# Two ends of a graph-network kernel: the last pair's output by plain products, against a prologue that loads its weights early

## The chip, the cores and the metric

The kernel runs on one core of one Trainium2 chip. The core has five instruction streams that run in parallel: TensorE (PE, matrix products into the accumulator memory PSUM), VectorE (DVE), ScalarE (ACT), GpSimd (POOL) and SyncE (SP, which here only issues transfers). Each stream runs its instructions strictly in order and waits on semaphores for the others. The metric is the device time of one execution in microseconds; the figure of a kernel is the median of its runs.

## The reference

128 graphs of 128 nodes go through two layers, each with a residual and a layer norm without scale or shift. `x` is [128, 128, 512], `adj` is [128, 128, 128] with zeros and ones. Everything is float32. Cut to what matters:

```python
# layer 0: graph attention, 8 heads of 64
feats = einsum('bnf,hfu->bhnu', X, W)                       # 512 -> 8 x 64
dense = leaky_relu(e_self[..., :, None] + e_neigh[..., None, :], 0.2)
dense = dense - 1e10 * (1 - A)
out   = relu(einsum('bhij,bhju->bhiu', softmax(dense), feats) + b)
x     = layernorm(x + out)

# layer 1: hypergraph convolution twice, with a layer norm between
def conv(x, adj, W, b):
    H  = (adj != 0)
    xw = einsum('ncd,hd->nch', x, W)
    return Dn * (H @ (Be * (H.T @ xw))) + b                 # = R @ xw + b
h = relu(conv(x, adj, W1, b1))                              # 512 -> 1024
h = layer_norm(h, gamma, beta)
y = conv(h, adj, W2, b2)                                    # 1024 -> 512
x = layernorm(x + (y + x))
```

`R` is one 128 x 128 matrix per graph. The kernel folds gamma, beta and the mean of `h` into W2 once, at the start; `bw` is the row that this leaves to add.

## The kernel before

Two graphs (a pair) are worked on together; there are 64 pairs. The three large products of a pair (features `pf`, hidden `ph`, output `py`) are made in the Strassen-Winograd manner: seven products of half size instead of eight, with sums of the operands made on VectorE or GpSimd and the results put together through copies of PSUM. The first two pairs use plain products for the features.

The whole program is a list of small steps. Each has a time (in units of the author's plan, not of the chip), and the steps are issued in the order of these times, so a time only sets where a step stands in each engine's stream:

```python
T = 38.6
for p in range(PAIRS):
    if p > 1:
        todo.append(({2: 81.0, 3: 131.0}.get(p, p * T), load, (p,)))
        ...
    for lag, time, name, since, fn, args in steps:
        ...
        time += (p + lag) * T
        todo.append((first.get((name, p) + args, first.get((name, p), time)), run, (fn, p, args)))
for _, fn, args in sorted(todo, key=lambda e: e[0]):
    fn(*args)
```

Names that the profile uses: `xb`, `ab` are blocks of x and adj as loaded, `a` and `w` the adjacency matrix and its first row on all partitions, `w_raw` the raw feature weights, `as_bc`, `an_bc` the attention vectors on all partitions; `pf` features, `ft` their copy; `rows`, `rd`, `nb` the neighbour terms, which go through DRAM to all partitions and become the scores; `nm` the negated maxima; `eT` the transposed exponentials; `pav` attention times features; `y` the first layer's output; `dd`, `dnb` the row factors, through DRAM; `pd` and `R` the propagator; `pz`, `zT` the propagated features and `zS` their sums; `phX`, `phY`, `phW` the hidden products; `h`, `hS` hidden values and their sums, `sq` their squares, `pm` the squares transposed; `pyX`, `pyY`, `pyW` the output products; `y2` (in the profile `y`) their result; `pq` the propagated output; `o` the result of the pair.

The start in this kernel: SyncE loads the first pair, the vectors and all weights ahead of the second pair's neighbour terms, and the row `gw` that W2 needs is spread by a small product:

```python
    load_blocks(0)
    load(0)
    load_edges(0)
    ...
    def prepare_output_spread():
        made["gw"], made["bw"] = (bank(n) for n in ("gw", "bw"))
        for c, n in enumerate(("gw", "bw")):
            nc.tensor.matmul(made[n], made["sel"][:, c, :], made["sums"], start=True, stop=True)
    ...
    todo = [
        ...
        (15.75, load_vectors, (0,)), (15.8, load_weights, (w1_blocks, w1t, F // 2, HALF)),
        (16.0, load_weights, (w2_blocks, w2t, DH // 2, QU)), (16.1, load_vectors, (1,)),
        (79.1, prepare_hidden, (nc.gpsimd, 0)), (79.2, prepare_hidden, (nc.gpsimd, 1)),
        (80.0, prepare_output_vectors, ()), (98.0, prepare_output, ()),
        (112.1, prepare_output_sums, ()), (117.75, prepare_output_spread, ()),
        ...
    first = {
        ("nodes", 0): 14.45, ...
        ("attend", 0): 97.85, ("attended", 0): 99.7, ("propagator", 0): 97.9, ...
        ("nodes", 1): 79.92, ...
        ("nodes", 2): 130.0, ... ("nodes", 3): 150.0, ...
    }
```

`prepare_output` makes `pv`, 16 small products of W2 (32 instructions in the profile) that lead to `gw` and `bw`; it needs `gbs`, made from gamma and beta. `nodes` makes the row factors of a pair from `a` and `w`. `w` has one buffer.

The end in this kernel: the last pair goes through the seven products like the others, with the sums of `h` on VectorE, and one store:

```python
    def h_sums(p, s, i):
        first_sums(s, "hS", f"hS_{p}", halves(s["h"], KH // 2), i,
                   nc.vector if p == PAIRS - 1 else nc.gpsimd, "hS")
    ...
    chain("py", 3, (24.2, 29.4, 27.7, 32.9, 31.2, 35.35, 37.1, 26.2, 29.6, 33.1), weigh, QU, 1)
    ...
    at(4, 10.9, output, 0)
    at(4, 11.8, output, 1)
    ...
    @step(4, 17.0)
    def o_norm(p, s):
        for g in range(2):
            normalize(s, "o", s["o"][:, g, :], g)
        nc.sync.dma_start(out[2 * p:2 * p + 2].rearrange("g n f -> n g f"), s["o"])
```

Of the kernel before, what the change touches and what calls it, by code (L numbers as in the profile page):

```python
# [20 lines left out]
def kernel(  # L21
# [82 lines left out]
    def load_blocks(p):  # L104
        s = st[p]
        gs = slice(2 * p, 2 * p + 2)

        s["xb"] = work.tile([P, 2 * NB, P], F32, tag="xb", name=f"xb_{p}")
        rows = x[gs].rearrange("g (b n) (f c) -> f n (g b) c", b=NB, f=NB)
        for f in range(NB):  # L110
            nc.sync.dma_start(s["xb"][f * B:(f + 1) * B], rows[f])

    def load_edges(p):
        s = st[p]

        s["ab"] = work.tile([P, 2 * NB, B], F32, tag="ab", name=f"ab_{p}")
        rows = adj[2 * p:2 * p + 2].rearrange("g (b n) (f e) -> f n (g b) e", b=NB, f=NB)
        for f in range(NB):
            nc.sync.dma_start(s["ab"][f * B:(f + 1) * B], rows[f])
# [22 lines left out]
    def everywhere(t, ap, queue):  # L142
        queue.dma_start(t, ap.partition_broadcast(P))

    as_bc, an_bc, b0_bc, b2_bc, bw_bc = (
        const.tile([P, F], F32, name=n) for n in ("as_bc", "an_bc", "b0_bc", "b2_bc", "bw_bc")
    )
# [3 lines left out]
    everywhere(as_bc, a_self, nc.scalar)  # L151
    everywhere(an_bc, a_neigh, nc.scalar)
    load_blocks(0)
    load(0)
    load_edges(0)

    def load_vectors(some):
        queue = nc.sync
        if some == 0:
            for t, ap in ((gb[:, 0, :], gamma), (gb[:, 1, :], beta)):  # L160
                queue.dma_start(t, ap.rearrange("(k p) -> p k", p=P))
            everywhere(b0_bc, b0, queue)
        else:
            queue.dma_start(b1_sb, b1.rearrange("(k p) -> p k", p=P))
            everywhere(b2_bc, b2, queue)
# [28 lines left out]
    def second_sums(engine, w, b12, some=slice(0, 4)):  # L194

        b11, b21, b22, t4, t1, t2, t3 = (w[i] for i in range(7))
        for dst, in0, in1 in ((t1, b12, b11), (t2, b22, t1), (t3, b22, b12), (t4, b21, t2))[some]:
            engine.tensor_tensor(dst, in0, in1, op=ALU.subtract)
# [13 lines left out]
    def prepare_first_sums():  # L212
        second_sums(nc.vector, [w0_sb[:, i] for i in range(7)], w0_12)

    def prepare_hidden(engine, i):
        a11, a12, a22, s1, s2, s3, s4 = (w1_sb[:, i] for i in range(7))
        dst, in0, in1, op = (
            (s1, w1_21, a22, ALU.add), (s2, s1, a11, ALU.subtract), (s3, a11, w1_21, ALU.subtract),
            (s4, a12, s2, ALU.subtract),
        )[i]  # L220
        engine.tensor_tensor(dst, in0, in1, op=op)
# [4 lines left out]
    def prepare_output_vectors():  # L226


        nc.vector.tensor_scalar(gbs[:, :, 0], gb[:, 0, :], 1.0 / DH, None, op0=ALU.mult)
        nc.vector.tensor_copy(gbs[:, :, 1], gb[:, 1, :])  # L230

        made["sel"] = work.tile([2, 2, P], F32, tag="y2", name="sel")
        nc.gpsimd.tensor_copy(
            made["sel"], ident[:2, :2].unsqueeze(2).to_broadcast([2, 2, P])
        )

    def prepare_output():
        pv = made["pv"] = [bank(f"pv{j}") for j in range(2)]
        for blk, i, j in w2_blocks:
            for k in range(KH // 2):  # L240
                nc.tensor.matmul(
                    pv[j][:2, :QU], gbs[:, i * KH // 2 + k, :], blk[:, k, :],
                    start=(i == 0 and k == 0), stop=(i == 1 and k == KH // 2 - 1),
                )

    def prepare_output_sums():
        made["sums"] = const.tile([2, F], F32, name="sums")
        for j in range(2):
            nc.scalar.copy(made["sums"][:, j * QU:(j + 1) * QU], made["pv"][j][:2, :QU])

    def prepare_output_spread():
        made["gw"], made["bw"] = (bank(n) for n in ("gw", "bw"))
        for c, n in enumerate(("gw", "bw")):
            nc.tensor.matmul(
                made[n], made["sel"][:, c, :], made["sums"], start=True, stop=True
            )

    def prepare_output_bias():
        nc.scalar.copy(bw_bc, made["bw"])
# [11 lines left out]
    def prepare_output_block_sums(engine, some):  # L271
        second_sums(engine, [w2_sb[:, i, :, :QU] for i in range(7)], w2_12, some)
# [5 lines left out]

    steps = []

    def step(lag, time, since=0):

        def keep(fn):
            steps.append((lag, time, fn.__name__, since, fn, ()))
            return fn
        return keep

    def at(lag, time, fn, *args, since=0):
        steps.append((lag, time, fn.__name__, since, fn, args))

    def chain(kind, lag, times, multiply, w, extra=0, since=0):
# [19 lines left out]
        for i, t in zip((1, 2, 6, 5, 7, 4, 3), times):  # L311
            at(lag, t, product, i, since=since)
        for i, t in enumerate(times[7:]):
            at(lag, t, copy, i, since=since)
# [473 lines left out]
    def squares(p, s, g, level):  # L788
# [3 lines left out]
        nc.gpsimd.tensor_tensor(t[:, :n, :], t[:, :n, :], t[:, n:2 * n, :], op=ALU.add)  # L792
# [5 lines left out]
    def h_sums(p, s, i):  # L798
        first_sums(s, "hS", f"hS_{p}", halves(s["h"], KH // 2), i,
                   nc.vector if p == PAIRS - 1 else nc.gpsimd, "hS")  # L800

    at(3, 20.9, h_sums, 0)
    at(3, 22.2, h_sums, 1)
    at(3, 19.6, h_sums, 2)
    at(3, 23.4, h_sums, 3)
# [3 lines left out]
    def weigh(s, i, to, start):  # L809
# [3 lines left out]
          QU, 1)  # L813
# [12 lines left out]
    at(3, 31.3, y_sum, 0, 0, 0, "Y")  # L826
    at(3, 34.9, y_sum, 1, 1, 2, "W")
    at(4, 0.1, y_sum, 0, 1, 1, "W")
    at(3, 37.2, y_sum, 1, 0, None, "X")

    @step(3, 34.8)
# [5 lines left out]
    @step(3, 36.0)  # L837
# [22 lines left out]
    at(4, 0.6, y_scale, 1)  # L860
    at(4, 1.3, y_scale, 0)
# [7 lines left out]
    at(4, 10.9, output, 0)  # L869
    at(4, 11.8, output, 1)  # L870
# [8 lines left out]
    at(4, 12.7, o_sum, 0)  # L879
    at(4, 13.3, o_sum, 1)  # L880
    at(4, 14.7, o_stats, 0)
    at(4, 15.5, o_stats, 1)
    at(4, 15.6, rstds, "o")

    @step(4, 17.0)
    def o_norm(p, s):
# [4 lines left out]

    T = 38.6
# [3 lines left out]
        (15.75, load_vectors, (0,)), (15.8, load_weights, (w1_blocks, w1t, F // 2, HALF)),  # L896
        (16.0, load_weights, (w2_blocks, w2t, DH // 2, QU)), (16.1, load_vectors, (1,)),
        (79.1, prepare_hidden, (nc.gpsimd, 0)), (79.2, prepare_hidden, (nc.gpsimd, 1)),
        (80.0, prepare_output_vectors, ()), (98.0, prepare_output, ()),
        (112.1, prepare_output_sums, ()), (117.75, prepare_output_spread, ()),  # L900
        (110.6, prepare_hidden, (nc.vector, 2)), (110.7, prepare_hidden, (nc.vector, 3)),
        (119.85, prepare_output_bias, ()),
        (117.8, prepare_output_blocks, (slice(0, 1),)),
        (118.1, prepare_output_blocks, (slice(1, 2),)),
        (122.0, prepare_output_blocks, (slice(2, 4),)),
        (126.5, prepare_output_block_sums, (nc.gpsimd, slice(0, 2))),
        (132.0, prepare_output_block_sums, (nc.vector, slice(2, 4))),
# [4 lines left out]
        ("nodes", 0): 14.45, ("write_nodes", 0): 14.5, ("spread_nodes", 0): 15.9,  # L912
        ("x_transpose", 0): 11.5, ("edges", 0): 15.2, ("scale_edges", 0): 15.4,
        ("spread_rows", 0): 13.5, ("neighbours", 0): 14.0, ("load_rows", 0): 14.2,
        ("attend", 0): 97.85, ("attended", 0): 99.7, ("propagator", 0): 97.9, ("r_evict", 0): 100.0,
        ("nodes", 1): 79.92, ("write_nodes", 1): 80.15, ("x_transpose", 1): 14.4,
        ("edges", 1): 110.4, ("scale_edges", 1): 110.5, ("spread_nodes", 1): 101.0,
        ("spread_rows", 1): 79.9, ("neighbours", 1): 80.1,
        ("propagator", 1): 117.76, ("r_evict", 1): 121.8,
        ("leaky", 1, 0, 0): 117.85, ("leaky", 1, 0, 1): 117.9, ("leaky", 1, 1, 0): 119.9,  # L920
        ("largest", 1, 0, 0): 118.0, ("largest", 1, 0, 1): 118.2, ("largest", 1, 1, 0): 120.2,
        ("masked", 1, 0, 0): 109.0,
        ("nodes", 2): 130.0, ("write_nodes", 2): 130.1, ("nodes", 3): 150.0,
        ("write_nodes", 3): 150.1, ("skip", 0): 128.5,
# [10 lines left out]
    for p in range(PAIRS):  # L935
        if p > 1:
            todo.append(({2: 81.0, 3: 131.0}.get(p, p * T), load, (p,)))
            todo.append((p * T + 19.0, load_blocks, (p,)))
            todo.append((p * T + 28.5, load_edges, (p,)))
        for lag, time, name, since, fn, args in steps:  # L940
            if p < since:
# [3 lines left out]
            if p == PAIRS - 1:  # L945
# [3 lines left out]
                    ("h_sums", 0): 19.1, ("h_sums", 1): 19.2,  # L949
                    ("product", 2): 25.0 if (lag, time) > (3, 20.0) else time,  # L950
                }.get((name,) + args[:1], time)
            time += (p + lag) * T
            todo.append((
                first.get((name, p) + args, first.get((name, p), time)), run, (fn, p, args)
            ))
# [46 lines left out]
```

## Time and profile before

| What | Value |
|---|---|
| Median of 3 runs | 2562.97 us (2560.83 to 2565.34) |
| Span of the profiled run | 2561.2 us |
| TensorE busy | 2513.8 us, 98% |
| VectorE, ScalarE, GpSimd busy | 83%, 59%, 67% |
| Moved by DMA | 345.04 MB, 135 GB/s on the mean |
| Time of one middle pair on TensorE | 38.67 us (pz at 2403.52, 2442.19 and 2480.85) |

The share of busy time is an average over the whole span. What the change touches lies in the first 100 and the last 65 us, so the profile is best read there: what each engine was idle for just before an instruction, and which chain of waits ended last. A line of the timeline gives the start and the duration in us, the engine and source line, the operation with its output and inputs, the count, and in brackets the idle time before it and what ended that.

### The profile page before, as it was taken

The page shows a single profiled execution, that of the slowest core. Times are in us where ns is not written, and L with a number is a line of the kernel's source. Part 1 is how long each engine was busy: PE and PEld are TensorE (multiplying, and loading weights), DVE is VectorE, ACT ScalarE, POOL GpSimd, SP SyncE. Part 2 cuts the span into 40 slices and gives each one's busy share as a digit, 9 for nine tenths or more (in the row PEclk, how much of TensorE's full clock was granted, in tenths as well). Part 3 has the DMA queues.
Part 4 walks back from the last instruction along what each step waited for, and adds up shares of the span by engine and source line. Part 5 has one row for each costly group of instructions (what it writes and reads, how often), then busy time and mean ns, then how long its engine had stood idle before and what let it go on. Part 6 is the DMA issues. An engine that isn't in the chain of part 4 may idle for free.

```text
span 2561.2 us, 48245 instructions
## 1 busy us (share of the span) xinstructions
PE 2513.8 (98%) x16316; PEld 2274.1 (89%) x16316; DVE 2128.5 (83%) x4644; ACT 1516.4 (59%) x4296; POOL 1722.1 (67%) x1802
## 2 busy tenths in 40 slices
PE   6899999999999999999999999999999999999997
PEld 4799999989989999999999998999999899998996
DVE  5788888888889888888888888888898888887875
ACT  3556656556556556556566566566565565565662
POOL 3676676766766766766766766767767666667653
PEclk8999999999999999999999999999999999999999
DMA  6444544454444444444444544444444444444430
GB/s 172 129 141 134 139 142 134 132 146 136 127 143 134 137 143 133 133 141 137 138 136 139 142 133 141 141 133 136 145 134 128 143 138 130 145 134 133 139 117 33
DMA packets 427958, 345.04 MB, mean 135 GB/s; under 512 B 146624, under 2 KB 377024, under 8 KB 427712
## 3 DMA queue, kind: packets, MB, share of 16 engines
q1 hardware_dynamic: 427424, 341.44, 45.4%
q8 instruction: 130, 2.13, 0.3%
q14 instruction: 116, 0.95, 0.1%
q10 hardware_dynamic: 288, 0.52, 0.1%
HBM read 240.14 MB, written 101.71 MB: 133 GB/s over the span
## 4 chain that ended last, share of the span: by engine, by line
PE 91%; DMA 3%; DVE 2%; issue 1%; POOL 1%; SPq 1%; ACT 0%; POOLq 0%; DVEq 0%
PE phX L741 18%; PE pyX L433 15%; PE phW L741 9%; PE pfX L433 9%; PE pyW L433 8%; PE pav L615 8%; PE phY L741 4%; PE pz L706 4%; PE pfW L433 4%; PE pq L865 4%; PE pyY L433 4%; PE pfY L433 2%; DMA nb<-rd 1%; PE pd L389 1%; DMA rd<-rows 1%
## 5 line engine op out<-in xcount | busy, mean ns | idle before, releaser
L741 PEld LDWEIGHTS phX<-zS,w_sb 128*128 128x128 f32 x3072 | 364.7, 193 | 39.4 <-issue 37.5
L535 POOL TENSOR_TENSOR nb<-nb,neg 128x512 f32<-128x512 f32 x256 | 321.3, 1277 | 111.7 <-DMA nb<-rd 65.4
L309 ACT COPY py<-pyX 128x257 f32<-128x257 f32 (+1 forms) x192 | 71.9, 374 | 547.9 <-PE pyX L433 544.7
L741 PE MATMUL phX<-zS,w_sb 128*128 128x128 f32 x3072 | 376.1, 276 | 8.8 <-issue 7.0
L792 POOL TENSOR_TENSOR sq<-sq 128x512 f32<-128x512 f32 (+2 forms) x384 | 343.5, 894 | 27.6 <-ACT sq L781 6.2
L542 ACT ACTIVATE nb<-nb,ft 128x128 f32<-128x128 f32 x1024 | 325.2, 390 | 27.5 <-POOL nb L535 25.5
L556 ACT ACTIVATE nb<-nb,nm 128x128 f32<-128x128 f32 x1024 | 320.2, 392 | 6.5 <-DVE nm L548 6.5
L662 POOL TENSOR_TENSOR rso<-veo,mhalf 128x2 f32<-128x2 f32 x64 | 44.9, 701 | 344.8 <-DVE veo L660 329.2
L646 DVE SCALAR_TENSOR_TENSOR y<-y,x 128x512 f32<-128x512 f32 x128 | 155.5, 1215 | 132.8 <-POOL y L639 132.8
L615 PEld LDWEIGHTS pav<-ft,eT 128*128 128x128 f32 x2048 | 253.5, 195 | 10.4 <-issue 1.9
L615 PE MATMUL pav<-ft,eT 128*128 128x65 f32 x2048 | 248.0, 275 | 2.1 <-DVE eT L577 1.6
L433 PE MATMUL pyX<-w_sb,hS 128*128 128x257 f32 (+1 forms) x1024 | 247.6, 384 | 2.2 <-DVE hS L415 1.8
L771 ACT ACTIVATE h<-h,b_sb 128x128 f32<-128x128 f32 x768 | 241.1, 391 | 11.4 <-DVE h L756 11.4
L433 PE MATMUL pyW<-w_sb,hS 128*128 128x256 f32 x1024 | 243.9, 380 | 3.7 <-DVE y L824 3.4
L433 PE MATMUL pyX<-w_sb,h 128*128 128x257 f32 (+1 forms) x1024 | 243.2, 379 | 0.0
L433 PEld LDWEIGHTS pyW<-w_sb,hS 128*128 128x128 f32 x1024 | 192.1, 189 | 36.6 <-DVE y L824 9.8
L433 PEld LDWEIGHTS pyX<-w_sb,hS 128*128 128x128 f32 x1024 | 189.9, 191 | 27.9 <-issue 2.1
L433 PEld LDWEIGHTS pyX<-w_sb,h 128*128 128x128 f32 x1024 | 189.2, 190 | 25.0
L639 POOL TENSOR_TENSOR y<-y,b_bc 128x512 f32<-128x512 f32 x128 | 162.3, 1268 | 61.5 <-DVE y L630 61.5
L548 DVE TENSOR_REDUCE nm<-nb 128x4 f32<-128x512 f32 x256 | 173.8, 679 | 8.6 <-ACT nb L542 6.0
L415 POOL TENSOR_TENSOR xS<-xT 128x256 f32<-128x256 f32 x124 | 118.0, 951 | 83.2 <-DVE xT L353 81.5
L309 ACT COPY ph<-phX 128x512 f32<-128x512 f32 x192 | 112.5, 586 | 94.4 <-PE phX L741 91.4
(136 smaller groups left out, 5828.8 us busy)
## 6 DMA issues: line engine op xcount, KB each, us to landing
nb<-rd SPq DMA_DIRECT2D x128, 512.0 KB, 6.4
ed<-nb SPq DMA_DIRECT2D x126, 512.0 KB, 3.2
eb<-ed SPq DMA_DIRECT2D x504, 128.0 KB, 2.9
xb<-in_x_dram SPq DMA_DIRECT2D x256, 128.0 KB, 3.0
x<-in_x_dram SPq DMA_DIRECT2D x64, 512.0 KB, 7.2
out_dram<-o SPq DMA_DIRECT2D x64, 512.0 KB, 2.9
a<-in_adj_dram SPq DMA_DIRECT2D x64, 128.0 KB, 6.5
w<-in_adj_dram SPq DMA_DIRECT2D x128, 64.0 KB, 4.3
```

Source lines behind the costliest of these rows:

```text
L309: nc.scalar.copy(t[:, :n], s[kind, "X"][:, :n])
L433: nc.tensor.matmul(to[:, :n], lhs[:, k, :], rhs[:, k, :n], start=bool(start) and k == 0, stop=(k == nk - 1), skip_group_check=True,)
L535: nc.gpsimd.tensor_tensor(t, t, neg[:, :, None, :].to_broadcast([P, NB, HH, B]), op=ALU.add)
L542: nc.scalar.activation(t, t, AF.Prelu, bias=s["ft"][:, g, h, 0:1], alpha=SLOPE)
L548: nc.vector.tensor_reduce(s["nm"][:, g, hs], scores(p, s, g, hs).rearrange("p b h j -> p h b j"), AX.XY, ALU.max, negate=True,)
L556: nc.scalar.activation(t, t, AF.Exp, bias=s["nm"][:, g, h:h + 1])
L615: nc.tensor.matmul(t[:, h * (U + 1):(h + 1) * (U + 1)], s["eT"][:, g, q * HH + h, :], s["ft"][:, g, q * HH + h, 2:], start=True, stop=True,)
L639: nc.gpsimd.tensor_tensor(s["y"][:, g, :], s["y"][:, g, :], b0_bc, op=ALU.add)
L646: nc.vector.scalar_tensor_tensor(y, y, 0.0, s["x"][:, g, :], op0=ALU.max, op1=ALU.add)
L741: nc.tensor.matmul(to[:, m * N:(m + 1) * N], w[:, k, m * P:(m + 1) * P], rhs[:, k, :], start=bool(start) and m == 0 and k == 0, stop=(k == ...
L771: nc.scalar.activation(dst[:, k, :], src[:, k, :], AF.Relu, bias=b1_sb[:, c:c + 1])
L792: nc.gpsimd.tensor_tensor(t[:, :n, :], t[:, :n, :], t[:, n:2 * n, :], op=ALU.add)
```

## The change

Its purpose is twofold. At the end, the last pair has no following work to hide its waits behind, so its output product is made by eight plain products per pair of halves instead of seven with sums, one graph after the other, and everything after it (row scaling, propagation, norm, store) goes by graph and by halves of 256 columns, so that one graph's rest lies beside the other's products. The pair before it makes its second output product ahead of the attention products and its sums of squares on VectorE. The last pair's store leaves by two queues.

At the start, this version has an earlier prologue in place of the one above: ScalarE issues the loads of the first pair's blocks and of the vectors, W2 is loaded ahead of W1, half of W1 comes behind the second pair's neighbour terms, `nodes` of pairs 1 and 2 stand earlier, all sums of weights are made on VectorE, `pv` stands between the two graphs' attention products, and `gw` and `bw` are spread through DRAM. The diff, cut to its core:

```diff
+    as_bc = everywhere(a_self, F, "as_bc")
+    an_bc = everywhere(a_neigh, F, "an_bc")
+    load(0)
+    load_blocks(0, nc.scalar)
+    load_edges(0, nc.scalar)
+    b0_bc = everywhere(b0, F, "b0_bc")
+    b2_bc = everywhere(b2, F, "b2_bc")
...
+    for t, ap in ((b1_sb, b1), (gb[:, 0, :], gamma), (gb[:, 1, :], beta)):
+        nc.scalar.dma_start(t, ap.rearrange("(k p) -> p k", p=P))
...
-    def prepare_output_spread():
-        made["gw"], made["bw"] = (bank(n) for n in ("gw", "bw"))
-        for c, n in enumerate(("gw", "bw")):
-            nc.tensor.matmul(
-                made[n], made["sel"][:, c, :], made["sums"], start=True, stop=True
-            )
...
+        sums_d = dram.tile([2, F], F32, tag="sums_d", name="sums_d")
+        nc.sync.dma_start(sums_d, sums)
+        gw = work.tile([P, F], F32, tag="y2", name="gw")
+        for c, t in ((0, gw), (1, bw_bc)):
+            nc.sync.dma_start(t, sums_d[c].partition_broadcast(P))
...
+        engine = nc.vector if p == LAST - 1 else nc.gpsimd
+        engine.tensor_tensor(t[:, :n, :], t[:, :n, :], t[:, n:2 * n, :], op=ALU.add)
...
+    def last_weights(p, s):
+        b12 = work.tile([P, KH // 2, QU], F32, tag="hS", name="b12")
+        nc.gpsimd.tensor_tensor(b12, w2_sb[:, 4, :, :QU], w2_sb[:, 0, :, :QU], op=ALU.add)
+        s["w2"] = ((w2_sb[:, 0], b12), (w2_sb[:, 1], w2_sb[:, 2]))
+    def last_weigh(p, s, g, j):
+        t = s["py", g, j] = bank(f"py_{g}{j}")
+        n = QU + (j == 0)
+        for i in range(2):
+            for k in range(KH // 2):
+                nc.tensor.matmul(t[:, :n], s["h"][:, g, i * KH // 2 + k, :], s["w2"][i][j][:, k, :n], ...)
...
+    def last_norm(p, s, g):
+        for j, queue in enumerate((nc.sync, nc.scalar)):
+            cols = slice(j * QU, (j + 1) * QU)
+            t = s["o"][:, g, cols]
+            nc.vector.tensor_scalar(t, t, s["mv", "o", g][:, 0:1], s["rs", "o", g], op0=ALU.subtract, op1=ALU.mult)
+            queue.dma_start(out[2 * p + g, :, cols], t)
+    for t, fn, *args in (
+        (8.0, last_weights),
+        (24.2, last_weigh, 0, 0), (27.8, last_weigh, 0, 1), (31.3, last_sum_squares, 0),
+        (31.4, last_h_rstd, 0), (31.5, last_weigh, 1, 0), (32.5, last_scale, 0, 0),
+        (32.6, last_scale, 0, 1), (34.9, last_sum_squares, 1), (35.0, last_h_rstd, 1),
+        (35.1, last_output, 0, 0), (35.2, last_output, 0, 1), (35.3, last_weigh, 1, 1),
+        (35.5, last_o_sum, 0, 0), ... (40.5, last_norm, 1),
+    ):
+        at(3, t, fn, *args, since=LAST)
...
-        (15.75, load_vectors, (0,)), (15.8, load_weights, (w1_blocks, w1t, F // 2, HALF)),
-        (16.0, load_weights, (w2_blocks, w2t, DH // 2, QU)), (16.1, load_vectors, (1,)),
+        (15.8, load_weights, (w2_blocks, w2t, DH // 2, QU)),
+        (16.0, load_weights, (w1_blocks[:2], w1t, F // 2, HALF)),
+        (80.2, load_weights, (w1_blocks[2:], w1t, F // 2, HALF)),
+        (103.0, prepare_output, ()), (116.5, prepare_output_sums, ()),
...
-        ("nodes", 2): 130.0, ("write_nodes", 2): 130.1, ("nodes", 3): 150.0,
+        ("nodes", 1): 17.6, ("write_nodes", 1): 17.9, ("x_transpose", 1): 14.5,
...
+            if p == LAST - 1:
+                time = {
+                    ("product", 2): 24.22 if (lag, time) > (3, 20.0) else time,
+                    ("squares", 0): 25.8, ("squares", 1): 28.0, ("h_sums", 2): 22.3,
+                }.get((name,) + args[:1], time)
```

## The prediction

> **What bounds the kernel now.** I began with the page: busy time, slices, chain that ended last.
>
> ```profile
> PE 2513.8 (98%) x16316; PEld 2274.1 (89%) x16316; DVE 2128.5 (83%) x4644; ACT 1516.4 (59%) x4296; POOL 1722.1 (67%) x1802
> ...
> PE 91%; DMA 3%; DVE 2%; issue 1%; POOL 1%; SPq 1%; ACT 0%; POOLq 0%; DVEq 0%
> ```
>
> The first line gives each engine's busy time, its share of the span and its instructions; the second, the share of each engine in the chain that ended last. TensorE (PE) is busy nearly throughout and is 91% of that chain, so only what stops TensorE counts. The change leaves the middle pairs alone, so I asked next for busy time by stretch: the stretch, its length, busy time and count for PE, weight loads, DVE (VectorE), ACT (ScalarE) and POOL (GpSimd), then granted clock, DMA share and GB/s.
>
> ```profile
> 0.00:50.00 50.00, 29.51 (x107) 23.19 (x107) 25.02 (x63) 16.56 (x45) 13.99 (x21) 0.87 0.63 162
> 50.00:100.00 50.00, 40.70 (x241) 32.44 (x240) 36.26 (x83) 23.63 (x67) 32.78 (x34) 0.89 0.55 149
> ...
> 150.00:200.00 50.00, 50.00 (x347) 46.26 (x346) 43.15 (x97) 33.71 (x97) 34.61 (x39) 1.00 0.41 125
> ...
> 2520.00:2562.00 42.00, 28.86 (x177) 23.99 (x175) 19.91 (x37) 10.56 (x28) 10.60 (x13) 0.93 0.07 26
> ```
>
> From 150 us on TensorE has no gap; it idles 20.5 + 9.3 = 29.8 us in the first 100 and 13.1 in the last 42. So a microsecond lost at the start is never made up, and each end counts in full. Then the timeline of both ends; these lines carry the working (start, duration, instruction, idle before):
>
> ```profile
> 14.65 3.86 PE L470 MATMUL pf<-w_sb,xT 128*128 128x264 f32 x8 [14.65 <-DVE xT L353]
> ...
> 32.36 4.94 POOL L535 TENSOR_TENSOR nb<-nb,neg 128x512 f32<-128x512 f32 x4 [18.05 <-DMA nb<-rd]
> ...
> 46.31 0.18 DVE L629 RECIPROCAL rden<-pav 128x4 f32<-128x4 f32 x1 [0.91 <-PE pav L615]
> ...
> 60.75 2.05 PE L706 MATMUL pz<-R,y 128*128 128x128 f32 x16 [0.50 <-ACT y L683]
> ...
> 83.35 3.75 PE L741 MATMUL phX<-zS,w_sb 128*128 128x128 f32 x16 [7.01 <-issue]
> ...
> 2500.23 6.01 PE L615 MATMUL pav<-ft,eT 128*128 128x65 f32 x32 [1.58 <-DVE eT L577]
> ...
> 2517.79 1.95 PE L706 MATMUL pz<-R,y 128*128 128x128 f32 x16
> ...
> 2533.84 1.90 PE L433 MATMUL pyX<-w_sb,h 128*128 128x257 f32 x8
> ...
> 2556.28 1.00 DVE L665 TENSOR_SCALAR o<-o,mvo,rso 128x512 f32<-128x512 f32 x2 [0.81 <-POOL rso L662]
> ```
>
> The 83.35 line is the last large hole of the start; from there to 2498 TensorE waits about 3 us in all (47.4 us idle in the span, less 29.8, 13.1 and the 1.58 at 2500). The 46.31 line is pair 0's first `attended`, which stands in the same place in both programs.
>
> **What the Trainium skill says.** "DMA: Bandwidth & Descriptors", section "Issuing engines are not separate DMA queues": transfers of all issuing engines run on the same 16 DMA engines; a second issuer saves only issue time. The trace agrees that the engines are the limit (share 0.98 at 295 GB/s in 4 to 8 us), so ScalarE's queue brings xb no sooner. "Perfetto Trace Analysis", section "DMA Instruction — HWDGE (DVE, Sync)": a DMA's semaphore wait is sat out by its issuing sequencer. The waits show it (engine and line, what it waited for, us in all, times, longest), where the third xb sits behind as_bc:
>
> ```profile
> SPq L111 <- DMA as_bc<-in_a_self_dram: 1.2, 1, 1.2
> ```
>
> That matters because xb and its followers now sit in ScalarE's own instruction stream.
>
> "TensorE: Matmul & The Clock Gate", section "What's actually happening": idleness halves the clock. The trace agrees in part: after the 1.58 us gap at 2500 it shows 0.50 from 2502 to 2508, after 1.78 us at 2539 it stays at 1.00. "GPSIMD Engine Reference", section "Engine selection": two-input elementwise work is about twice as slow there. Here 128x512 takes 1.27 us on GpSimd, 0.69 to 1.65 on VectorE, the more the busier GpSimd is beside it.
>
> **The start: what goes back, step by step** (in brackets the time before; estimates from the rows named, while the order of instructions in the changed program, and what each waits for, say who follows whom).
>
> 1. ScalarE must now issue 13 more DMAs (xb, ab, biases, gamma, beta) before its table load and weight copies. They reuse eight landing semaphores, so the third xb waits for raw weights (landed 8.4), b2 for that xb (another 5 to 6), gamma and beta for ab. ScalarE is free near 16 (8.4 + 5.5, then four issues of 0.5); table load 1.28, first copy 0.62: 17.9. The first product starts there, not at 14.65: **+3.3**. GpSimd's mask add (32.36) moves to 35.7.
> 2. Pair 1's `nodes` now stands ahead of pair 0's maxima on VectorE and waits for w, issued about 34, 5 us to land: 39.4. Plus its 1.3 us, maxima start at 40.7 (35.03 before); exponentials end at 47.7 (43.24): **+1.2** more. First pav 48.8 (44.31).
> 3. Pair 2's `nodes` now stands ahead of pair 0's `attended`. Its w follows six weight blocks, 3.1 MB: from 39 at the 383 GB/s seen at 42 to 46 us, till 47. The small dd write behind lands about 49; SyncE waits for it before dnb; then a and w, 5 us: 55. `nodes` ends, `attended` starts at 56.3 (46.31): **+5.5** more.
> 4. TensorE makes the 32 pv instructions between the graphs' pav (7.9 us, 52.36 to 60.24 before; there they hid a wait for y). gbs comes behind `attended`, so pv runs 58 to 66, pav and pd 3.9 more: 69.9. Then graph 1's attended, bias, residual, statistics, rstd and shift, 0.9+1.3+0.7+1.1+0.9+0.3, and 0.8 for y, in the durations of the same rows. pz starts at 76.0 (60.75): **+5.2** more.
> 5. Eight leaky activations (2.5 us) stand ahead of zT, so the first hidden product starts at 80.4 (65.19). The sums stay late: +15.2.
> 6. gw now goes through DRAM. The copies of its sums stand on VectorE behind the four hidden sums (4 x 1.2) and two maxima, which begin at 77 when the leaky activations have been made: 84. Write 2.6 (a dd write's landing), broadcast read 5.3: 92.3. Eight scalings 3.3, maximum 0.7, exponentials 1.3, ph copy 0.6, all in order: the held product starts at 98.2 (83.35), +14.9. The 7 us hole stays, only 15 us later.
> 7. VectorE makes all eight second-product and hidden sums (GpSimd made four). Two of 1.2 us delay eT behind them, so the next pav waits about **2** more.
>
> Sum at the start: **+17**, 11 to 21.
>
> **The end: what is gained.** From pz of the last pair the order is unchanged up to the weighting, 16.05 us later. Then plain products: 16 k-blocks per graph, each 1.73/4 = 0.43, so 13.8 us against 12.1 for the seven, but without the 1.78 and 0.47 us waits. From pz as zero: weigh(0,0) 16.05, (0,1) 19.5, transpose 22.97, weigh(1,0) 23.1, its transpose and graph 0's output 26.6, weigh(1,1) 27.6 to 31.05. Graph 0's variance, rstd and both scalings (0.7+0.8+1.0) lie beside weigh(1,0); its sums, statistics and half its norm beside weigh(1,1). Left after it: scale 0.6, output and wait 0.7, two half sums and statistics 1.3, aggregate to rstd 1.4, two half norms 0.7, issue and landing 2.9, finish 1.1: about 39.7. Now it is 2561.2 - 2517.8 = 43.4. Gain: **3.7**.
>
> Before it, the last but one: its second product fills the 1.58 us gap ahead of pav, and a pav at full clock takes 3.46, not 6.01, the next product 1.79, not 2.83. That is 5.2 us. But its squares are now on VectorE, and the second graph's stand behind attended, two residuals, statistics and shift. VectorE walked: eT to 2501.9, attended 0 to 2503.1, first squares beside GpSimd's sums to 2506, attended 1 to 2507.4, first residual 1.74 (the duration beside GpSimd), statistics 0.9, second residual and statistics 1.6, rstd and shift 1.5: 2513. I get the last square at 2513 to 2514.5, while TensorE is at the transpose by 2509.9. It waits 3 to 4.5 us, and the clock may fall. I put pz where it was, give or take 3. The two moves **nearly cancel**.
>
> Net: 17 - 3.7 - 0 = +13; I take 1.5 off, as some of steps 2 to 4 wait for the same DMAs, and say **2574.5 us**.
>
> **Rivals.** (a) The start costs little: the weights land while TensorE has other work, GpSimd mask and exponentials hide the rest. For it: DMA share is only 0.5 to 0.6 over the first 100 us. Against: engines run in order and the two early `nodes` stand right in pair 0's chain. It would make +4 at the start, 2563 or so. (b) The end gains all 8.9 us because squares on VectorE are quick (0.7+0.4+0.25) and no wait follows. For it: GpSimd is freed of 5.7 us just there. Against: order on VectorE. It would make about 2569. (c) VectorE becomes the bound after the start, since sums pile up and pair 1's softmax runs late; it is at 83% already. That would make 2580 or more.
>
> **Range and chances.** Start +11 to +21, end -9 to 0; these hardly go to extremes together: 2565 to 2583. Two per cent is 51 us, thrice the largest sum: within 2% 0.98, slower 0.02, faster 0.
>
> **What would show it.** Right: first pf product near 18; a VectorE wait on a w DMA just ahead of the first reciprocal, to 55; pz of pair 0 near 76; the phX hole ending near 98, gw's landing ahead of it; full TensorE from about 150; at the end no gap ahead of the last pav, a wait at the transpose pm behind VectorE's squares, and 40 us from last pz to end. Wrong: if the phX hole ends before 92, the DMA chain of step 3 was overrated; if pm waits under 1 us, the squares were; if the middle shows gaps, rival (c).

## The result, and the profile after

The changed kernel takes 2585.5 us (median of 6 runs, 2581.3 to 2587.4), the kernel before 2562.6 us on the same chips: a ratio of 1.0086, 95% interval 1.0073 to 1.0099. The change costs 23 us; 2574.5 (2565 to 2583) was predicted. The direction was right; the size was 11 us too small, and 2585.5 lies above the upper end of the range. The trace shown here is of a run at the upper end, 2587.4 us, with a span of 2585.5.

Read in the same order as before: first the page (busy time, chain that ended last).

```profile
PE 2515.8 (97%) x16324; PEld 2274.8 (88%) x16324; DVE 2140.6 (83%) x4661; ACT 1514.7 (59%) x4291; POOL 1714.4 (66%) x1794
...
PE 89%; DMA 4%; DVE 3%; issue 2%; POOL 1%; ACT 0%; SPq 0%; ACTq 0%; POOLq 0%; DVEq 0%
```

TensorE's busy time is as before (2513.8). What was added is idle time, and the chain names DMA and VectorE a little more. Busy time by stretch says where (columns as in the prediction: stretch, length, busy time and count of PE, weight loads, DVE, ACT, POOL, then clock, DMA share, GB/s):

```profile
0.00:50.00 50.00, 19.23 (x64) 15.00 (x64) 18.21 (x43) 7.95 (x19) 12.12 (x23) 0.92 0.67 162
50.00:100.00 50.00, 34.14 (x184) 25.51 (x184) 31.32 (x70) 20.47 (x60) 15.26 (x15) 0.70 0.45 115
100.00:150.00 50.00, 42.99 (x268) 38.94 (x269) 45.53 (x99) 27.95 (x81) 30.41 (x29) 0.93 0.40 118
150.00:200.00 50.00, 50.00 (x325) 45.52 (x324) 41.89 (x92) 29.57 (x83) 36.21 (x37) 1.00 0.48 138
```

TensorE is full from 150 us, as predicted, but idles 30.8 us in the first 50 (20.5 before) and 15.9 in the next (9.3). The mean clock of the second stretch is 0.70. The timeline of the start names the waits (in brackets the idle time just before, and what ended it; SPq is SyncE's queue):

```profile
19.72 3.89 PE L455 MATMUL pf<-w_sb,xT 128*128 128x264 f32 x8 [19.72 <-ACT w_sb L196]
37.82 4.94 POOL L520 TENSOR_TENSOR nb<-nb,neg 128x512 f32<-128x512 f32 x4 [23.58 <-DMA nb<-rd]
44.35 9.23 SPq L324 DMA_DIRECT2D dd_d<-dr  x2
53.00 0.21 DVE L319 STREAM_TRANSPOSE dr<-dn 128x32 f32<-128x32 f32 x1 [9.09 <-DMA dd_d<-dr]
53.13 1.85 DVE L533 TENSOR_REDUCE nm<-nb 128x4 f32<-128x512 f32 x3
54.33 2.48 PE L574 MATMUL pet<-ident,nb 128*128 128x128 f32 x8 [13.47 <-issue]
62.86 0.18 DVE L614 RECIPROCAL rden<-pav 128x4 f32<-128x4 f32 x1 [1.03 <-PE pav L600]
84.89 3.78 PE L691 MATMUL pz<-R,y 128*128 128x128 f32 x16 [7.92 <-ACT y L668]
105.91 3.76 PE L726 MATMUL phX<-zS,w_sb 128*128 128x128 f32 x16 [7.07 <-issue]
117.78 2.00 PE L600 MATMUL pav<-ft,eT 128*128 128x65 f32 x16 [0.36 <-DVE eT L562]
```

The same places in the kernel before:

```profile
29.68 0.41 SPq L339 DMA_DIRECT2D dd_d<-dr  x1
35.03 0.69 DVE L548 TENSOR_REDUCE nm<-nb 128x4 f32<-128x512 f32 x1 [4.50 <-ACT nb L542]
37.78 2.33 PE L589 MATMUL pet<-ident,nb 128*128 128x128 f32 x8 [2.20 <-POOL neg L343]
45.06 0.21 DVE L334 STREAM_TRANSPOSE dr<-dn 128x32 f32<-128x32 f32 x1
93.74 1.90 PE L615 MATMUL pav<-ft,eT 128*128 128x65 f32 x16
```

The line to see is the one at 53.00. A transpose of 0.21 us, the last instruction of pair 1's `nodes`, stood 9.09 us because it writes `dr`, which has one buffer, and pair 0's row factors in it were still on their way to DRAM: SyncE came to that 16 KB write at 44.35, behind six weight blocks, and it landed 8.6 us later (the 9.23 of its line also hold pair 1's write, which waited for the transpose). In the kernel before the write went out at 29.68, ahead of the weights, and pair 1's transpose at 45.06 waited for nothing. Two rows of the table of times do this: the changed kernel has 16.5 for pair 0's write (14.5 before) and its weights at 15.8 and 16.0, and it has 17.6 for pair 1's `nodes` (79.92 before). Pair 0's maxima are next in VectorE's order, so they started at 53.13 instead of 35.03, and TensorE idled 13.47 us ahead of pair 0's transposes. The prediction had neither this wait nor the 13.47.

The end, in the same view:

```profile
2527.78 3.68 PE L600 MATMUL pav<-ft,eT 128*128 128x65 f32 x32
...
2541.06 0.47 PE L820 MATMUL pm<-ident,sq 128*128 128x128 f32 x1 [3.44 <-DVE sq L778]
2541.32 3.41 PE L418 MATMUL pyX<-w_sb,h 128*128 128x256 f32 x8
...
2546.30 1.95 PE L691 MATMUL pz<-R,y 128*128 128x128 f32 x16
```

The same eight instructions in the kernel before:

```profile
2514.32 1.90 PE L433 MATMUL pyX<-w_sb,h 128*128 128x256 f32 x8
```

No gap ahead of the last attention products now (1.58 before) and 3.68 us for them instead of 6.01; in exchange 3.44 of waiting for VectorE's squares, and behind it eight instructions that took 3.41 instead of 1.90. From the last `pz` to the end 39.2 us (43.4 before).

So the 24.3 us between the two traces fall into: start up to the second pair's first attention product 24.0 (93.74 to 117.78), middle 3.5, last but one pair 1.0, end -4.2.

### The profile page after: what moved, and what is told of

Same layout as the page of the kernel before. It is cut to its first block, busy times and chain, and to the rows that moved or that the text cites. A ratio compares the mean times of both kernels' runs of the same rounds, so it can differ in the third digit from the quotient of the medians.

```text
span 2585.5 us, 48274 instructions
## 1 busy us (share of the span) xinstructions
PE 2515.8 (97%) x16324; PEld 2274.8 (88%) x16324; DVE 2140.6 (83%) x4661; ACT 1514.7 (59%) x4291; POOL 1714.4 (66%) x1794
## 4 chain that ended last, share of the span: by engine, by line
PE 89%; DMA 4%; DVE 3%; issue 2%; POOL 1%; ACT 0%; SPq 0%; ACTq 0%; POOLq 0%; DVEq 0%
PE phX L726 18%; PE pyX L418 14%; PE phW L726 9%; PE pfX L418 9%; PE pyW L418 8%; PE pav L600 8%; PE phY L726 4%; PE pz L691 4%; PE pfW L418 4%; PE pq L850 4%; PE pyY L418 3%; DMA nb<-rd 2%; PE pfY L418 2%; PE pd L374 1%; DMA rd<-rows 1%
## 5 line engine op out<-in xcount | busy, mean ns | idle before, releaser
L294 ACT COPY py<-pyX 128x257 f32<-128x257 f32 x189 | 70.8, 374 | 537.5 <-PE pyX L418 537.5
L778 POOL TENSOR_TENSOR sq<-sq 128x512 f32<-128x512 f32 x378 | 339.3, 898 | 32.4 <-ACT sq L766 11.6
L418 PE MATMUL pyX<-w_sb,hS 128*128 128x257 f32 x1008 | 242.6, 382 | 0.6 <-ACT py L294 0.6
L418 PE MATMUL pyX<-w_sb,h 128*128 128x257 f32 x1008 | 240.9, 381 | 0.0
L418 PEld LDWEIGHTS pyW<-w_sb,hS 128*128 128x128 f32 x1008 | 189.0, 189 | 39.2 <-DVE y L809 12.8
```

Of the source, the lines that this page charges most:

```text
L294: nc.scalar.copy(t[:, :n], s[kind, "X"][:, :n])
L418: nc.tensor.matmul(to[:, :n], lhs[:, k, :], rhs[:, k, :n], start=bool(start) and k == 0, stop=(k == nk - 1), skip_group_check=True,)
L778: engine.tensor_tensor(t[:, :n, :], t[:, :n, :], t[:, n:2 * n, :], op=ALU.add)
```

## Experiments

Each run is compared with runs of the kernel before on the same chip; these had medians from 2562.5 to 2566.0, so where runs of different sets are compared the ratios are the safer figures. "Old start" is the prologue of the kernel before. The steps of the start, as predicted and as measured, in us; the first product varied from 17.3 to 19.7 over ten traces with the changed prologue, so the columns are to be compared within some 2 us.

| | before | predicted | after | e1 | e3 | e7 |
|---|---|---|---|---|---|---|
| first feature product | 14.65 | 17.9 | 19.72 | 18.39 | 17.36 | 18.33 |
| maxima of pair 0 | 35.03 | 40.7 | 53.13 | 41.38 | 41.00 | 41.44 |
| first attended | 46.31 | 56.3 | 62.86 | 58.10 | 50.74 | 51.16 |
| pz of pair 0 | 60.75 | 76.0 | 84.89 | 78.22 | 72.08 | 68.35 |
| end of the phX hole | 83.35 | 98.2 | 105.91 | 99.27 | 94.71 | 92.03 |
| next pav | 93.74 | hole + 12.4 | 117.78 | 111.13 | 106.57 | 103.88 |
| whole (median) | 2562.6 | 2574.5 | 2585.5 | 2579.5 | 2576.0 | 2570.7 |

(e1: two buffers for `dr`; e3: that and late `nodes` of pair 2; e7: that and `pv` behind the attention products.)

### e1, e2, e3: the wait for dr, and the one behind it

```diff
# e1
-        s["dr"] = work.tile([P, B], F32, tag="dr", name=f"dr_{p}")
+        s["dr"] = work.tile([P, B], F32, tag="dr", name=f"dr_{p}", bufs=2)
# e2 (on the changed kernel); e3 has both
+        ("nodes", 2): 111.0, ("write_nodes", 2): 111.1,
```

e1: 

> The changed kernel with two buffers for dr, so that pair 1's transpose of its row factors need not wait until pair 0's row factors have been written behind six weight blocks. Theory A (this wait of 9.1 us is what the prediction missed, and nothing stands behind it): maxima of pair 0 start at 44 (53.1), first attended at 53 to 54 (62.9), pz of pair 0 at 76 (84.9), the whole about 2576. Theory B (the wait for pair 2's w, which the prediction put at this place, takes over, since w is issued only after dnb, whose source lands at 53): maxima at 44, TensorE's gap ahead of the transposes of pair 0 shrinks to about 4, but nodes of pair 2 wait for w until about 60 and the first attended starts at 61 to 62; pz at 83 to 84, the whole within 2 of the changed kernel's.

e2: 

> The changed kernel with nodes of pair 2 (and the write of its row factors) moved behind pair 0's attended and first shift, dr still with one buffer. Both theories: the dr wait stays, so maxima still start at 53, first attended about 1.1 to 1.3 earlier than 62.9 at most (the time of nodes alone), pz of pair 0 at 83.5 to 85, the whole within 2 of the changed kernel's.

e3: 

> Both edits of the two runs before at once. Theories A and B: maxima at 44, first attended at 53 to 54, pz of pair 0 at 75 to 76, the hole ahead of the held hidden product ends at 97 (105.9), the whole at 2576 to 2577. If the delay were instead made good later (gw through DRAM or the sums on VectorE set the end of the hole whatever comes before), pz would be at 76 but the hole would still end at 102 or later and the whole stay above 2581.

Measured: e1 2579.5 us (ratio 1.0064, 1.0047 to 1.0080); e2 2584.0 in a single run; e3 2576.0 (1.0047, 1.0032 to 1.0062). VectorE's timeline of e1:

```profile
41.38 1.85 DVE L533 TENSOR_REDUCE nm<-nb 128x4 f32<-128x512 f32 x3
...
56.82 0.29 DVE L310 SCALAR_TENSOR_TENSOR w<-a,w 128x128 f32<-128x128 f32 x1 [7.98 <-DMA w<-in_adj_dram]
...
58.10 0.14 DVE L614 RECIPROCAL rden<-pav 128x4 f32<-128x4 f32 x1
```

With the second buffer the maxima start at 41.38, and 8 us of waiting appear where there was none: pair 2's `w`, just ahead of the first `attended`. That is the wait that the prediction had put there. Both waits hang on one landing, that of pair 0's dd write: SyncE issues dnb, and behind it pair 2's `a` and `w`, only when it is there (dnb goes out at 50.70 in e1, at 53.68 in the changed kernel). In the changed kernel VectorE, held until 53.0 itself, had maxima, sums and copies to make first; it came to `w` at 60.51, and by then `w` was there. Taking away the second wait alone (e2) gains next to nothing: its maxima still start at 50.13, and from first product to next pav it takes 98.7 (98.1 in the changed kernel). Taking away both gains 9.5. Theory B held in kind; e1 gained 6, between its 2 and theory A's 9.5, because `w` landed at 57 and not at 60. No run put the dd write back ahead of the weights, which might have met both waits at their source.

### e4: who issues the first loads

```diff
-    load(0)
-    load_blocks(0, nc.scalar)
-    load_edges(0, nc.scalar)
+    load_blocks(0)
+    load(0)
+    load_edges(0)
...
+        (15.75, load_vectors, (0,)), (16.1, load_vectors, (1,)),   # biases, gamma, beta by SyncE
```

> The changed kernel with the loads of the first pair's blocks and of all vectors issued by SyncE as in the kernel before; ScalarE issues only as and an. Step 1 of the prediction in its measured size: first product at 14.7 to 15 (19.7), mask add at 32.5 to 33 (37.8), everything behind about 5 earlier unless SyncE's longer queue gives it back: pz of pair 0 at 80, the whole at 2580 to 2581. Rival (the dr and w waits hang on SyncE's queue and weights, which now has 7 more loads ahead of dd): first product at 15, but maxima at 51 or later, the whole above 2583.

Measured: 2582.8 us (1.0077, 1.0061 to 1.0093). The first product, and the same transpose:

```profile
12.45 3.86 PE L459 MATMUL pf<-w_sb,xT 128*128 128x264 f32 x8 [12.45 <-DVE xT L342]
```

```profile
50.06 0.21 DVE L323 STREAM_TRANSPOSE dr<-dn 128x32 f32<-128x32 f32 x1 [14.18 <-DMA dd_d<-dr]
```

The start begins 7 us earlier, and the wait for `dr` grows from 9.1 to 14.2. The maxima start only 2.9 earlier, and about that is gained (2.8, with intervals that overlap those of the changed kernel): nearer to the rival than to the theory. SyncE now has the first loads and the vectors ahead of the dd write as well and comes to it at 45.31, no sooner than in the changed kernel (44.35). What ScalarE's issuing costs in front is mostly lost again in the wait behind SyncE's loads.

### e7, e8: the order behind attended

```diff
# e7, on e3
-        (103.0, prepare_output, ()),
+        (105.2, prepare_output, ()),
# e8, on e3
-        (122.4, prepare_output_blocks, (slice(0, 2),)),
+        (123.2, prepare_output_blocks, (slice(0, 2),)),
```

e7: 

> The run with two buffers for dr and late nodes of pair 2, and in addition pv behind both graphs' attention products, as in the kernel before, instead of between them. Step 4 of the prediction (pv between them delays graph 1's output, and there it hides nothing): pz of pair 0 at 65 (72.1), the hole ends at 88 (94.7), the whole at 2569 to 2570. Rival (VectorE's queue of sums and W1's second half, which land when they land, set the end of the hole): pz at 65, hole still ends at 92 or later, the whole at 2573 or more.

e8: 

> The run with two buffers for dr and late nodes of pair 2, and in addition the first eight scalings of W2 by gw (4.8 on VectorE) behind pair 1's last maximum instead of ahead of it. Theory O (the order on VectorE makes the hole: maximum, exponentials and ph copy stand behind the scalings): hole ends at 90 (94.7), next pav at 102 (106.6), the whole at 2571 to 2572. Theory V (the amount of VectorE's work up to the next pav makes the delay): hole ends at 90, but the scalings now stand ahead of the transposed exponentials, next pav still at 105 to 106.6, the whole at 2575 to 2576. If gw's way through DRAM set the end of the hole, it would not move with VectorE's order at all only if the scalings started at gw's landing; they start at once behind a sum there, so this is held unlikely.

Measured: e7 2570.7 us (1.0025, 1.0013 to 1.0036), e8 2574.5 (1.0044, 1.0030 to 1.0058). With `pv` behind both graphs' attention products, pz comes at 68.35, 50.0 behind the first product instead of 54.7: step 4's 5.2, measured 4.7 at pz, and 5.4 in the whole. The end of the hole, measured the same way, comes 3.7 earlier. In e8 (TensorE's timeline):

```profile
90.87 3.75 PE L726 MATMUL phX<-zS,w_sb 128*128 128x128 f32 x16 [3.67 <-POOL xS L400]
96.93 3.78 PE L726 MATMUL phW<-zT,w_sb 128*128 128x128 f32 x16 [2.30 <-DVE h L741]
...
107.19 2.00 PE L600 MATMUL pav<-ft,eT 128*128 128x65 f32 x16 [0.36 <-DVE eT L562]
```

The hole ends 4 us earlier, at 90.87, and the next pav comes no sooner, at 107.19: the scalings only moved from ahead of the maximum to ahead of `h` and `eT`. Theory V held. From the shift of pair 0 to the next pav VectorE has hardly a gap; in e7, by the columns of the stretches above:

```profile
66.20:104.00 37.80, 24.47 (x159) 21.51 (x158) 36.96 (x75) 20.78 (x61) 19.39 (x17) 0.86 0.58 144
```

It is busy 36.96 of 37.80 us, so its order there only moves the wait from one product to the next.

### e9, e10, e13: taking work off that stretch

```diff
# e9, on e7
-        (112.0, prepare_hidden, (0,)), (112.5, prepare_hidden, (1,)),
-        (130.6, prepare_output_block_sums, (slice(0, 2),)),
+        (112.0, prepare_hidden, (nc.gpsimd, 0)), (112.5, prepare_hidden, (nc.gpsimd, 1)),
+        (130.6, prepare_output_block_sums, (slice(0, 2), nc.gpsimd)),
# e10, on e9
-        ("nodes", 1): 17.6, ("write_nodes", 1): 17.9,
+        ("nodes", 1): 79.92, ("write_nodes", 1): 80.15,
# e13, on e7 (all sums stay on VectorE)
-        (80.2, load_weights, (w1_blocks[2:], w1t, F // 2, HALF)),
-        (112.0, prepare_hidden, (0,)), ... (115.0, prepare_hidden, (3,)),
+        (16.05, load_weights, (w1_blocks[2:], w1t, F // 2, HALF)),
+        (108.75, prepare_hidden, (0,)), ... (108.9, prepare_hidden, (3,)),
```

e9: 

> The run with pv behind the attention products (and two buffers for dr, late nodes of pair 2), and in addition two of the four hidden sums and two of the four output block sums on GpSimd, as in the kernel before. Theory V (from pz of pair 0 to the second pair's attention product VectorE works without a gap, so what is taken from it is gained in full): 4 x 1.2 = 4.8 less, next pav at 99 (103.9), the whole at 2566. Rival (GpSimd's own mask adds are now late and slow VectorE's two-input work beside them): next pav at 102 or later, the whole at 2568.5 or more.

e10: 

> The run with half the sums on GpSimd, and in addition nodes of pair 1 behind pair 0's maxima, as in the kernel before. Theory: maxima of pair 0 need no longer wait for pair 1's w and start with the mask add, 3 to 4 earlier relative to the first product; everything behind moves along: the whole at 2562.5. Rival: VectorE gets nodes back in the middle of its gapless stretch, or pair 1's w and rows come later, so 0 to 1 is gained: 2565 or more.

e13: 

> The run with pv behind the attention products (two buffers for dr, late nodes of pair 2), and in addition all of W1 loaded ahead of the second pair's neighbour terms, and the four hidden sums, still on VectorE, in the gap of 5.1 us in which it waited for rsa. Theory V in its narrower form (VectorE's gapless stretch from pair 1's first maximum to the next pav sets the delay; the run with sums on GpSimd lost because GpSimd then sat out W1's load ahead of the operands zS): 4.8 less in the stretch, next pav at 99 to 100 (103.9), the whole at 2566. Rival (the earlier load holds up dd, w and nb of pair 1 by some 3): next pav at 102 or later, the whole at 2569 or more.

Measured: e9 2578.5 us (1.0049, 1.0034 to 1.0064), slower than e7, by far more than the rival's reason (mask adds beside VectorE) had led to expect; e10 2577.8 (1.0047, 1.0034 to 1.0061); e13 2572.1 (1.0029, 1.0018 to 1.0040). GpSimd's timeline of e9:

```profile
72.22 3.43 POOL L215 TENSOR_TENSOR w_sb<-w,w_sb 128x1024 f32<-128x1024 f32 x1 [3.08 <-DMA w_sb<-in_w1t_dram]
75.73 2.34 POOL L215 TENSOR_TENSOR w_sb<-w_sb 128x1024 f32<-128x1024 f32 x1
78.02 1.26 POOL L520 TENSOR_TENSOR nb<-nb,neg 128x512 f32<-128x512 f32 x1
79.25 1.38 POOL L328 TENSOR_SCALAR neg<-a 128x256 f32<-128x256 f32 x1
80.60 0.72 POOL L714 TENSOR_TENSOR zS<-zT 128x256 f32<-128x256 f32 x1
```

In e9 the sums have new company. GpSimd waits 3.08 for W1's second half, works 5.8 on two sums (2.9 on VectorE in e7), and only then comes to the operands zS, at 80.60 instead of 72.37. The first hidden product that uses them stood 6.75 us. In the kernel before all of W1 was loaded ahead of this, which the changed kernel no longer does. Later VectorE's own sums, beside GpSimd's work, took 3.07 and 2.28 us (1.21 and 1.47 in e7), and the next pav waited 2.80 for eT and came at 106.27 (103.88). That is the rival's kind of reason in another place, so this run does not tell how much W1's late load costs and how much GpSimd's work as such. Of the 10.3 us between the traces of e7 and e9, 5.7 are there at pair 1's pz (122.15 and 127.86); 4.8 lie in the middle pairs, which e9 does not change. e10 had its maxima 3.6 earlier (38.00; 0.9 of it from an earlier first product) and gained little: the same hidden product stood 6.91 there.

e13 gives the sums a gap of VectorE instead. From the shift to the next pav it takes 31.9 us (37.7 in e7), so work taken out of the stretch is gained there, and a wait of 1.8 for `gw` appears in it:

```profile
84.14 2.06 DVE L250 SCALAR_TENSOR_TENSOR w_sb<-w_sb,gb,gw 128x256 f32<-128x256 f32 x4 [1.82 <-DMA gw<-sums_d]
```

But the earlier load of W1 delays what follows it: pair 1's mask add starts at 67.28 (64.26), the shift behind it at 70.29 (66.23). The two nearly cancel, and the ratio is that of e7. The rival held in the sum, theory V in its stretch.

### e14: gw by product

```diff
# on e7
-        nc.sync.dma_start(sums_d, sums)
...
-            nc.sync.dma_start(t, sums_d[c].partition_broadcast(P))
+            nc.tensor.matmul(b, sel[:, c, :], made["sums"], start=True, stop=True)
+            nc.scalar.copy(t, b)
```

> The run with pv behind the attention products, and in addition gw and bw spread by two small products and two ScalarE copies instead of through DRAM. Step 6 as the prediction put it (gw's way through DRAM, 2.6 + 5.3, stands in the chain to the hole's end): hole ends 3 to 4 earlier than 92.0, the whole at 2567. Rival (gw lands when VectorE comes to the scalings anyway; the wait for it was 0.2): hole ends at 91.5 to 92.5, the whole at 2570 to 2571.

Measured: 2571.8 us (1.0020, 1.0009 to 1.0031), hole end 91.54 (92.03 in e7). The way through DRAM costs nothing that can be seen here, because VectorE comes to the scalings no sooner than `gw` lands: they start at 84.28 without a wait, and at 84.89 in e7 after one of 0.22.

### e5, e6, e11, e12: the end with the old start

e5 is the old start with the whole changed end. e12 leaves the last but one pair as in the kernel before. e6 and e11 change the table of the last but one pair further:

```diff
# e12, on e5: squares on GpSimd, and
-            if p == LAST - 1:
-                time = {...}
# e6, on e5
+                    ("sum_squares",): 39.55, ("h_rstd",): 39.6, ("y_scale", 1): 1.05,
# e11, on e6
-                    ("squares", 0): 25.8, ("squares", 1): 28.0,
+                    ("squares", 0): 37.4, ("squares", 1): 37.45,
```

e5: 

> The prologue of the kernel before, with the changed end (last pair by plain products, last but one's moves). Theory: the two parts add up, so this is the kernel before less what the end gave in the changed kernel's trace (4.2 from last pz to end, less 1.0 ahead of it): 2559.3, first 100 us as in the kernel before, a wait of 3.4 at the transpose pm. Rival: the short waits of the output products for VectorE between 120 and 2500 us (4.6 in all after, 1.8 before) come with the changed end's program and not with the start: then 2562.

e12: 

> The kernel before with the last pair's new output alone; the last but one pair as in the kernel before (squares on GpSimd, second product where it was). The prediction's claim that the last but one's two moves cancel: a gap of 1.5 ahead of pav and half clock behind it come back, the wait at pm goes; from its last hidden product to pz 22.8, the whole within 1 of the run with the changed end entire (2559.8). Rival: the moves help or hurt by more than 2, then under 2558 or over 2562.

e6: 

> As the run before, and in addition the last but one pair's transposes of the squares, its row scale and what hangs on it stand behind the last pair's propagation pz instead of ahead of two output products. Theory: the wait of 3.4 at pm and the half clock behind it (1.5) go, pz waits for y alone: from the last but one's last hidden product to pz 18.5 to 19.5 instead of 23.8, the whole at 2554.5 to 2555. Rival: y is late too, since VectorE makes the squares ahead of the shift's followers, so only 1 to 2 are gained: 2557.5.

e11: 

> The old prologue, the changed end, pm behind pz (the run before of that kind), and in addition both graphs' squares of the last but one pair behind the additions of its output sums on VectorE, so that attended, y and these additions come 2 to 3 earlier. Theory: the wait of 2.3 for y's addition at pyW goes down to under 0.5, pz 2 earlier, pm behind pz waits for nothing: the whole at 2555.5 to 2556. Rival: pm behind pz now waits for the squares (over 1), or first layer output y comes no sooner because GpSimd's bias adds hold it: the whole at 2557 to 2558.

Measured: e5 2559.8 us (0.9985, 0.9979 to 0.9992), e12 2560.2 (0.9981, 0.9974 to 0.9988), e6 2557.9 (0.9979, 0.9971 to 0.9987), e11 2557.5 (0.9970, 0.9959 to 0.9982). e5 and e12 do not differ: the last but one's two moves are worth nothing together, as predicted, and the last pair's new output is worth 0.15 to 0.19%, 4 to 5 us. The gap ahead of pav is there in e12 and the wait at pm in e5, each with slower products behind it (pav in 4.72 us, 3.68 in e5; in e5 eight instructions in 3.14, 1.90 in e12):

```profile
2503.64 4.72 PE L616 MATMUL pav<-ft,eT 128*128 128x65 f32 x32 [1.57 <-DVE eT L578]
```

```profile
2513.29 0.48 PE L836 MATMUL pm<-ident,sq 128*128 128x128 f32 x1 [3.15 <-DVE sq L794]
```

e6 takes the wait at pm away and meets the next one, in TensorE's timeline:

```profile
2513.97 1.97 PE L434 MATMUL pyW<-w_sb,hS 128*128 128x256 f32 x8 [2.29 <-DVE y L825]
```

In e11 the squares stand behind the additions that this product waits for:

```profile
2498.50 1.95 PE L742 MATMUL phW<-zT,w_sb 128*128 128x128 f32 x16
...
2515.10 1.97 PE L434 MATMUL pyW<-w_sb,hS 128*128 128x256 f32 x8
2516.91 1.95 PE L707 MATMUL pz<-R,y 128*128 128x128 f32 x16
```

From the last but one's last hidden product to pz 18.4 us, against 20.8 in e6, 23.2 in e5 and 22.8 before. That is the step expected; in the whole it shows less (the intervals of e6 and e11 overlap). e11 is faster than both kernels, than the kernel before by 0.3% (0.2 to 0.4).

## Why the prediction was right and wrong

**Wrong: step 2.** It let VectorE wait for pair 1's `w` only (39.4; 41.64 in the trace) and start the maxima 1.3 us later, at 40.7; they started at 53.13. The missed term is the single buffer of `dr`: 9.1 us. The prediction knew that the small dd write stands behind the weights (it used its landing in step 3, for dnb, and put it at 49; it was 53.0) but did not ask which buffer that write holds, and who writes it next. Had it asked, the steps would have stood as in e1, where they hold: maxima 41.38 for 40.7, attended 58.10 for 56.3, pz 78.22 for 76.0, hole end 99.27 for 98.2, and the start up to the next pav costs 17.4 for 17. e1 and e3 show the cause: 6 us for the buffer alone, 9.5 with the wait that takes its place. Between the two traces 24.3 us were lost where 11.8 had been summed. Of the 12.5 missed, 6.6 are this wait (the next pav at 117.78, at 111.13 in e1; 1.3 of it is the first product's own difference), 3.5 lie in the middle, 1.5 had been taken off as overlap, and 0.9 are the rest.

**Step 3** (pair 2's `w`, +5.5) was right in e1 (a wait of 8.0), and in the changed kernel it was hidden: what the prediction said would show there, a wait for a `w` just ahead of the first reciprocal, is not in its trace. The two waits, 9.1 and 8.0, do not add up: without both, 9.5 were gained. The prediction took 1.5 off for waits on the same DMAs, but from a sum in which the larger one was missing.

**Step 1** was right as a time (17.9; ten traces 17.3 to 19.7), and worth less than it looks: e4 won 7 us there (12.45) and 2.8 in the end. What the Trainium skill says under "Issuing engines are not separate DMA queues" ("DMA: Bandwidth & Descriptors"), that a second issuer saves only issue time, agrees: here it saved none and delayed ScalarE's own work.

**Step 4** was right: 5.2 for pv, 4.7 measured at pz, 5.4 in the whole (e7). **Step 5**'s time from pz to the first hidden product, 4.4, was met as well (84.89 to 89.32).

**Step 6** had the right size for the wrong reason. The hole stayed 7 us long and came as late as all else, but not through DRAM (e14): the amount of VectorE's work from pair 0's shift to the next pav sets it (e8, and the stretch of e13; there, with the four sums gone, 1.8 of `gw`'s way showed). **Step 7** named this and put it at 2; e1 shows 1.5 more than before from hole to next pav.

**The end**: 3.7 predicted, 4.2 in the trace, 3.7 in the whole with the old start (e5). **The last but one**: predicted to cancel, with a wait of 3 to 4.5 at pm; measured 3.44 and a loss of 1.0 (e5 and e12: no difference).

**Rivals.** (a) did not come. (b), the 8.9 of the end in full, did not come from the change, but e11 shows that most of it was there once pm and the squares were moved: 8.0 against the kernel before. (c) was half right: VectorE is the bound up to the next pav (busy 31.69 of the 32 us from 86 to 118 in the changed kernel), not afterwards: TensorE has no gap in the 42 us behind it. By the prediction's own sign, gaps in the middle would also speak for (c); they are there, but small, and the next paragraph leaves their cause open.

**Open.** The middle cost 3.5 more in the trace: short waits of the output products for VectorE's additions, 4.6 us in all against 1.8 before. With the old start they sum to 3.1 (e5), 3.8 (e11) and 4.8 (e12) between 118 and 2500 us, so the changed start does not bring them. Whether the changed end's program does, or whether they scatter from run to run, is not shown: there is one trace of each kernel, and over these sixteen traces the time from pair 1's pz to that of the last but one pair goes from 2366.9 (the kernel before) to 2377.0 us (e9), with 2372.2 in the changed kernel. The 3.5 may be scatter in part.

## What to carry to other kernels

When instructions of a later pair are moved forward, list for each not only what it reads but what it writes: a one-buffer tile whose last reader is a small transfer behind large ones can hold its next writer until that transfer lands, here for 9 us and 16 KB. Look also at what was put ahead of such a transfer. Where one wait is removed, look for the next one that ends almost as late; here the second took back 3.5 of the 9.5 us until both were gone. And where one engine works without a gap, changing its order moved the wait (e8), and moving its work to an engine that waited for a transfer itself, and slowed the first one beside it, made the whole 6 to 8 us longer (e9; by ratio and by median).

## What was not expected

The first product 7 us earlier (e4) made a later wait 5 us longer, and 2.8 us were left in the whole. GpSimd took 3.43 and 2.34 us for sums that VectorE made in 1.2 to 1.75 (e9, e7), while the first of them ran beside VectorE's own work. TensorE's granted clock was 0.50 from 2541 to 2544, behind a gap of 3.44 us (3.41 us for eight instructions). In e6 it stayed at 1.00 behind a gap of 2.29 us (1.97 us for eight), yet in the kernel before it was 0.50 from 2502 to 2508, behind a gap of 1.58 us; how long a gap has to be is not settled by these runs.
